# Even and odd sums made after the transposes; six of twelve row tiles kept transposed in DRAM for the rotation

## The chip, the cores and the metric

The kernel runs on one core of a Trainium2 chip. The metric is the device time of one launch in microseconds (us), as the median of several runs. The engines are called TensorE (PE in the profile, with PEld for its weight loads), VectorE (DVE), ScalarE (ACT), GpSimd (Pool) and SyncE (SP), which only issues DMAs here. Each takes its own instructions in order and waits on semaphores for the others.

## The reference

Eight images of 256 channels and 96 x 96 pixels go through two residual layers, all in float32:

```python
x = x + _L0_conv_ref(_gn(x), ...)     # group norm, then attention in the Fourier domain
x = x + _L1_conv_ref(_gn(x), ...)     # group norm, then linear attention
```

Layer 0 makes q, k and v by 256 x 256 matrices over the channels, takes a two-dimensional FFT of each, normalises every channel of q and k over all frequencies, forms 32 x 32 attention matrices per head and takes the softmax of their real and imaginary parts apart:

```python
attn = jnp.einsum('bhcn,bhdn->bhcd', q_f, k_f) * temperature
attn = complex(softmax(real(attn)), softmax(imag(attn)))
out = abs(ifft2(einsum('bhcd,bhdn->bhcn', attn, v_f)))
return pconv(out, w_out)
```

Layer 1 projects x to 32 channels of q and k with softplus, sums k times v over all pixels, and divides q times that sum by q times the sum of k.

## The kernel before, in words

No FFT is computed. The products of q and k over all frequencies without conjugation are, in space, products of x with x mirrored in both axes. So layer 0 needs two 256 x 256 matrices of the image, the second moments of its even part (x plus x mirrored) and of its odd part (x minus x mirrored). The imaginary part of the attention needs a second image y, which is x with every pair of a row and its columns turned by a fixed table of 96 x 96 for each row ("rotation").

One image x lies in an arena of SBUF, channels on 128 partitions in two halves (`KC = 2`), in twelve tiles of 8 rows (`NT`). A tile t holds four rows from the top and the four that mirror them (`x_col`), so a tile carries its own mirror, and tile 0 also the row 48, which mirrors itself. The second arena holds y, and is given to the next image in turn. `ring` (4 buffers of 1536 elements), `three` (3 buffers), `one` and `xT` (6 slots of 2 x 258) are SBUF buffers; `psum` has five banks for all transposes and products but the long sums.

The stages of one image are Python generators, woven together so that TensorE gets work of one stage while another waits:

- `pair_sums(b)`: L313 to L318 add and subtract the mirrored halves of a tile on VectorE or Pool (`even_odd`), L350 transposes 128 pixels of both (4 transposes, "eoT"), L353 copies them to `xT` on ScalarE, and L331 adds their products with themselves to the two sums ("acc"). The products of a step are issued one step behind its transposes. There are 37 steps for an image: three for each of twelve tiles, and one for row 48. `stats_chunk` takes the statistics of the group norm along the way.
- `attention(b)` turns the two sums into the matrices of the heads, a chain of small products and steps of VectorE and ScalarE. Its `yield n` says how many steps of rotation go between its pieces.
- `rotate(b)`: a step takes two rows. L550 transposes each row (2 transposes a row, "xr"), L563 copies them to `xT` on ScalarE, and two steps later L553 multiplies them by the row's table ("y", two passes for each float32 product), and L558 and L559 copy row sums and y from PSUM on VectorE. The table of six rows is a tile "tm", read as overlapping windows of the DRAM tensor `rt` (576 pieces of 384 bytes), with a last column put in by Pool (L536).
- `images(b)`: the products z (L621), squares and roots on VectorE, ScalarE and Pool, and the projection po (L633), added to x.
- `layer1(b)` and `output(b)`: layer 1 in the same arena; L779 transposes x again ("xT"), L782 and L784 copy it on ScalarE or VectorE. `output` adds the result to x on VectorE (L868) and, for one of four pieces, on ScalarE and Pool (L871, L872), and stores it (L882).

`weave` runs image b's attention with its own rotation; `pair_sums(b + 1)` is woven into `images(b)`, `layer1(b)` and `output(b)`, and what is left follows bare. Every stage issues the loads of the next image on SP as space comes free. Where `tc.manual_schedule` names an engine, its instructions stand in the order of the program; elsewhere a planner orders them by when it thinks that they are ready. Attention and rotation have TensorE's order by hand; output and the rest of the sums have TensorE, VectorE, Pool and SP by hand, and ScalarE by the planner; images and layer1 have all by the planner. The sums of the first image stand alone at the start, with VectorE by hand.

Of the kernel before, what the change touches and what calls it, by code (L numbers as in the profile page):

```python
# [54 lines left out]
KC = 2  # L56
# [3 lines left out]
TR = 6  # L60
NZ = 33
# [7 lines left out]
def two_layer_kernel(ctx: ExitStack, tc: tile.TileContext, x, w1t, b1, w2t, b2, w3, b3, wot, temp,  # L69
# [96 lines left out]
    turn = [0, 0]  # L166

    def xt_slot(sums=False):

        turn[sums] += 1  # L170
        return xT[:, NX - 2 + turn[1] % 2 if sums else turn[0] % (NX - 2)]
# [8 lines left out]
    half = const.tile([P, 1], F32, name="half")  # L180
    nc.vector.memset(half, 1.0)
    nc.vector.memset(half[0:W], 0.5 ** 0.5)
# [46 lines left out]
    rt = dram.tile([H, 2 * W], F32, name="rt")  # L229

    def tables():

        nc.vector.reduce_sum(rep4[:, 0:D], ident.rearrange("p (j d) -> p d j", d=D), axis=AX.X)
        for j in range(1, 4):
            nc.vector.tensor_copy(rep4[:, 32 * j:32 * j + 32], rep4[:, 0:D])
        nc.vector.tensor_copy(sel8.rearrange("p (i d) -> p i d", d=D), rep4[:, 0:8].unsqueeze(2).to_broadcast([P, 8, D]))
        for j in range(4):
            o = HEAD * j
            nc.vector.tensor_copy(gsel[:, 0:16, j], gri[:, o:o + 16])
            nc.vector.tensor_copy(gsel[:, 17:32, j], gri[:, P + o + 1:P + o + 16])  # L240
            nc.vector.tensor_copy(gsel[:, 32, j:j + 1], gri[:, o + 16:o + 17])
        pcs = ps_tile("pcs")
        for c in range(2):
            nc.tensor.matmul(pcs[0:H, c:c + 1], lhsT=csn[0:1, c, :], rhs=ones[0:1, 0:1], start=True, stop=True)
        cs = t0[:, 5 * W:5 * W + 2]
        nc.vector.tensor_copy(cs, pcs[0:H, 0:2])
        r0 = t0[:, 2 * W:3 * W]
        nc.vector.tensor_scalar_mul(t0[:, 0:W], t0[:, 0:W], cs[:, 0:1])
        nc.vector.scalar_tensor_tensor(r0, in0=t0[:, W:2 * W], scalar=cs[:, 1:2], in1=t0[:, 0:W], op0=ALU.mult, op1=ALU.add)
        for i in range(2):  # L250
            o = (3 + i) * W
            nc.vector.tensor_copy(t0[:, o:o + 1], r0[:, 0:1])
            nc.vector.tensor_copy(t0[:, o + 1:o + W], r0[:, W - 1:0:-1])
        nc.sync.dma_start(out=rt, in_=t0[:, 3 * W:5 * W])
        load_small()

    def window(h):

        v = rt[h:h + TR, 1:1 + W]
        return bass.AP(v.tensor, v.offset, [[1, W], [2 * W, TR], [1, W]])  # L260
# [35 lines left out]
    def even_odd(b, u):  # L296

        assert (b, u % NT) in loaded
        nr = PR if u < NT else 1
        t = ring_tile(f"eo_{b}_{u}").rearrange("p (c k n) -> p c k n", c=2, k=KC)  # L300
        x_t = image(x_of(b))
        rows = [PR * u + i for i in range(nr)]
        if u in (0, NT):
            parts = [(0, 1)] + ([(1, nr)] if nr > 1 else [])
        else:
            parts = [(0, nr)]
        for lo, hi in parts:
            n = hi - lo
            ra = x_col(rows[lo]) // W
            rp = x_col((H - rows[lo]) % H) // W  # L310
            back = slice(rp, rp - n if rp >= n else None, -1)
            for c in range(2):
                eng = nc.vector if u in (0, 1, NT) or (u == NT // 2 - 1 if b else u % 2) else nc.gpsimd  # L313
                op = (eng.tensor_add, eng.tensor_sub)[c]
                pop = (nc.gpsimd.tensor_add, nc.gpsimd.tensor_sub)[c]
                d = t[:, c, :, 0:nr * W].rearrange("p k (h w) -> p k h w", w=W)
                op(d[:, :, lo:hi, 1:W], x_t[:, :, ra:ra + n, 1:W], x_t[:, :, back, W - 1:0:-1])  # L317
                pop(d[:, :, lo:hi, 0:1], x_t[:, :, ra:ra + n, 0:1], x_t[:, :, back, 0:1])  # L318
        return t, nr * W

    s0 = {}

    def pair_sums(b):

        st0 = new_stats(f"st0_{b}")
        acc = [acc_tile(f"acc{c}_{b}") for c in range(2)]

        def products(t, np_, first, last):
            for c in range(2):
                for m in range(KC):  # L330
                    mm = nc.tensor.matmul(acc[c][:, m * C:m * C + (KC - m) * P], lhsT=t[0:np_, c, m * P:(m + 1) * P],  # L331
                                          rhs=t[0:np_, c, m * P:C], start=(first and m == 0), stop=(last and c == 1),
                                          skip_group_check=True)
                    if first and m:
                        tc.keep_in_program_order(mm)

        pending, first = None, True
        us = [*range(NT - 1, -1, -1), NT]
        ahead = [even_odd(b, us.pop(0))]
        for u in range(NT - 1, -2, -1):  # L340
            u %= NT + 1
            eo, cols = ahead.pop(0)
            for i in range(0, cols, P):
                while i == 0 and us and len(ahead) < (2 if b and u in (NT - 3, NT - 4) else 1):
                    ahead.append(even_odd(b, us.pop(0)))
                np_ = min(P, cols - i)
                pt = ps_tile(f"eoT_{b}_{u}_{i}")
                for c in range(2):
                    for k in range(KC):
                        nc.tensor.transpose(pt[0:np_, c * C + k * P:c * C + (k + 1) * P], eo[:, c, k, i:i + np_], ident)  # L350
                t = xt_slot(True)
                weight = half[0:np_] if u in (0, NT) and i == 0 else 1.0
                nc.scalar.activation(t[0:np_, :, 0:C], pt[0:np_, :].rearrange("p (c n) -> p c n", c=2), AF.Copy,  # L353
                                     scale=weight)
                if pending is not None:
                    products(*pending, first, False)
                    first = False
                pending = (t, np_)
                if u < NT and i:
                    stats_chunk(st0, b, 2 * (NT - 1 - u) + i // P - 1)  # L360
                yield
        s0[b] = st0, acc, products, pending
# [4 lines left out]
    def attention(b):  # L367
        st0, acc, products, pending = s0.pop(b)
        wl = ring_tile(f"wl_{b}").rearrange("p (k o) -> p k o", k=KC)
        nc.sync.dma_start(out=wl[:, :, 0:C], in_=w1t.rearrange("(k p) o -> p k o", p=P))  # L370
        nc.sync.dma_start(out=wl[:, :, C:2 * C], in_=w2t.rearrange("(k p) o -> p k o", p=P))
        nc.sync.dma_start(out=wl[:, :, 2 * C:3 * C], in_=w3.rearrange("(k p) i -> p k i", p=P))
# [14 lines left out]
        yield 2  # L387
# [80 lines left out]
        yield 3  # L468

        for m in range(KC):  # L470
# [15 lines left out]
            yield (5, 3)[m]  # L486
# [38 lines left out]
    def rotate(b):  # L525
# [6 lines left out]

        def load_r(h):
            tm = three.tile([P, TR * (W + 1)], F32, tag="tm", name=f"tm_{b}_{h}")[0:W].rearrange("p (r w) -> p r w", r=TR)
            (nc.scalar if b else nc.sync).dma_start(out=tm[:, :, 0:W], in_=window(h))
            nc.gpsimd.tensor_copy(tm[:, :, W:W + 1], csn[0:W, 2, h:h + TR].unsqueeze(2))  # L536
            return tm

        def step(h, turned):
# [3 lines left out]
            if turned is not None:  # L543
                g, gt, tm = turned
                pu = ps_tile(f"y_{b}_{g}")
            for r in range(2):
                for k in range(KC):
# [3 lines left out]
                    if turned is not None and g + r:  # L551
                        o = (r * KC + k) * (W + 1)
                        nc.tensor.matmul(pu[:, o:o + W + 1], lhsT=gt[0:W, r, k * P:(k + 1) * P], rhs=tm[:, g % TR + r, :],  # L553
                                         start=True, stop=True)
            if turned is not None:
# [3 lines left out]
                nc.vector.tensor_copy(y[:, :, :, g + r:g + 2], src[:, :, W - 1::-1, r:2])  # L559
            if h is not None:  # L560
                xt = xt_slot()
                r = 0 if h else 1
                nc.scalar.copy(xt[0:W, r:2, 0:C], pt[0:W, r * C:2 * C].rearrange("p (r n) -> p r n", n=C))  # L563
                return xt

        tms = [load_r(g) for g in range(0, 3 * TR, TR)]
        pending = []
        for h in range(0, H, 2):
            if h % TR == 0:
                tm = tms.pop(0)  # L570
            if h % TR == 4 and 3 * TR <= h - 4 + 2 * TR < H:
                tms.append(load_r(h - 4 + 2 * TR))
            xt = step(h, pending.pop(0) if len(pending) == 2 else None)
            pending.append((h, xt, tm))
# [5 lines left out]
    st1s = {}  # L580

    def images(b):
# [26 lines left out]
        nc.vector.tensor_mul(sg[2], sg[2], sg[2])  # L609

# [69 lines left out]
    def layer1(b):  # L680
# [72 lines left out]
        def add_kx(i, xt, kT):  # L753
# [4 lines left out]
        extra = [three.tile([P, TR * (W + 1)], F32, tag="tm", name=f"xt{i}_{b}")[:, 0:2 * (C + 2)].rearrange(  # L758
            "p (j n) -> p j n", j=2) for i in range(2)]
        for t in extra:  # L760
            nc.gpsimd.memset(t[:, :, C:C + 2], 1.0)
        slots = [*(xT[:, i] for i in range(4)), *extra]
        pend = []
        softplus(0, 0)
        for s in range(NS):
# [6 lines left out]
            for i in range(s * CH // P, (s + 1) * CH // P):  # L772
                xt = [slots[2 * (i % 3) + jj] for jj in range(2)]
                for jj in range(2):
# [6 lines left out]
                    if jj or i % 3 == 2:  # L781
# [116 lines left out]
    with tc.manual_schedule(engines={mybir.EngineType.DVE}):  # L898
# [67 lines left out]
```

## Time and profile before

| | us |
|---|---|
| median of 3 runs (2762.49 to 2765.9) | 2763.46 |
| the profiled execution | 2762.53 |
| its span, first to last instruction | 2760.7 |
| one image to the next, from the first z at 1170.5 to that at 1509.8 | 339.3 |
| TensorE transposes xr (L550), number | 1520 |
| TensorE passes y (L553), number | 3040 |

The page gives busy time of the engines, the chain of work that ended last, and groups of instructions by source line. The stages of the image in the middle lie at 1170 to 1300 us (images), to 1382 (layer1), to 1432 (output and the bare sums) and to 1510 (attention and rotation). Matmuls overlap in the array, so a mean duration of a matmul is longer than the time from one to the next; the pace is read from starts. "eoT", "acc", "xr" and so on are the names of the tiles that a group writes.

### The profile page before, as it was taken

The page shows a single profiled execution, that of the slowest core. Times are in us where ns is not written, and L with a number is a line of the kernel's source. Part 1 is how long each engine was busy: PE and PEld are TensorE (multiplying, and loading weights), DVE is VectorE, ACT ScalarE, POOL GpSimd, SP SyncE. Part 2 cuts the span into 40 slices and gives each one's busy share as a digit, 9 for nine tenths or more (in the row PEclk, how much of TensorE's full clock was granted, in tenths as well). Part 3 has the DMA queues.
Part 4 walks back from the last instruction along what each step waited for, and adds up shares of the span by engine and source line. Part 5 has one row for each costly group of instructions (what it writes and reads, how often), then busy time and mean ns, then how long its engine had stood idle before and what let it go on. Part 6 is the DMA issues. An engine that isn't in the chain of part 4 may idle for free.

```text
span 2760.7 us, 47785 instructions
## 1 busy us (share of the span) xinstructions
PE 2719.5 (99%) x18348; PEld 1972.5 (71%) x18348; DVE 1958.4 (71%) x4104; ACT 1366.5 (49%) x2098; POOL 841.5 (30%) x939
## 2 busy tenths in 40 slices
PE   8999999999999999999999999999999999999988
PEld 8965679657795677956679566885678856788556
DVE  7588666876668767587675875769766687676776
ACT  3455634556345563355634546345453455544553
POOL 5033340342403423035230351313513135131311
PEclk9999999999999999999999999999999999999997
DMA  5120151201512015120151201521015210251003
GB/s 169 40 65 11 47 184 43 67 9 49 179 43 73 6 47 182 43 69 6 54 179 46 63 6 54 182 54 52 7 53 184 58 46 7 62 178 28 0 7 138
DMA packets 197274, 192.50 MB, mean 70 GB/s; under 512 B 88821, under 2 KB 197049, under 8 KB 197049
## 3 DMA queue, kind: packets, MB, share of 16 engines
q1 hardware_dynamic: 129800, 164.34, 18.8%
q10 hardware_dynamic: 67248, 25.12, 3.6%
q8 instruction: 146, 2.39, 0.4%
q14 instruction: 80, 0.65, 0.1%
HBM read 113.85 MB, written 75.57 MB: 69 GB/s over the span
## 4 chain that ended last, share of the span: by engine, by line
PE 94%; DVE 3%; ACT 2%; DMA 1%; issue 1%; POOL 0%; SPq 0%; POOLq 0%; DVEq 0%; ACTq 0%
PE z L621 21%; PE po L633 18%; PE acc L331 13%; PE y L553 10%; PE xr L550 6%; PE eoT L350 5%; PE xT L779 5%; PE kq L718 5%; PE o L863 4%; PE kx L755 3%; DMA arena<-in_x_dram 1%; PE cw L423 1%; PE kT L770 1%; DVE arena L559 1%; PE mz L511 1%
## 5 line engine op out<-in xcount | busy, mean ns | idle before, releaser
L621 PE MATMUL z<-arena,mz 128*128 128x384 f32 (+2 forms) x2400 | 595.0, 476 | 0.0
L633 PE MATMUL po<-e,wo 128*128 128x384 f32 x1536 | 529.7, 486 | 0.2 <-ACT e L668 0.2
L667 POOL TENSOR_TENSOR e<-e 128x768 f32<-128x768 f32 x192 | 348.2, 1815 | 554.1 <-ACT e L666 554.1
L621 PEld LDWEIGHTS z<-arena,mz 128*128 128x128 f32 (+1 forms) x2400 | 325.6, 163 | 241.4 <-issue 42.4
L553 PE MATMUL y<-tm,xT 96*128 96x97 f32 x3040 | 472.6, 261 | 1.7 <-ACT sd_a L288 0.5
L553 PEld LDWEIGHTS y<-tm,xT 96*128 96x128 f32 x3040 | 457.8, 192 | 12.5 <-issue 4.9
L331 PE MATMUL acc<-xT 128*128 128x256 f32 (+2 forms) x2368 | 440.5, 328 | 3.5 <-ACT xT L353 3.5
L633 PEld LDWEIGHTS po<-e,wo 128*128 128x128 f32 x1536 | 289.4, 190 | 197.7 <-DVE arena L635 1.2
L662 DVE TENSOR_TENSOR e<-z,xT 128x768 f32<-128x768 f32 x384 | 365.7, 953 | 85.2 <-PE z L621 85.2
L264 DVE BATCH_NORM_STATS2 st<-arena 128x6 f32<-128x384 f32 x768 | 406.5, 552 | 13.7 <-DMA arena<-in_x_dram 3.2
L550 PE MATMUL xr<-ident,arena 128*96 128x128 f32 x1520 | 409.2, 275 | 0.0
L331 PEld LDWEIGHTS acc<-xT 128*128 128x128 f32 (+1 forms) x2368 | 380.2, 191 | 37.7 <-ACT xT L353 5.2
L563 ACT COPY xT<-xr 96x512 f32<-96x512 f32 (+1 forms) x384 | 220.2, 578 | 293.8 <-PE xr L550 289.4
L666 ACT ACTIVATE e<-e 128x1536 f32<-128x1536 f32 x192 | 284.6, 1482 | 93.5 <-DVE e L662 92.3
L668 ACT ACTIVATE e<-e 128x768 f32<-128x768 f32 x192 | 161.9, 843 | 334.0 <-POOL e L667 332.9
L317 POOL TENSOR_TENSOR eo<-arena 128x760 f32<-128x760 f32 x136 | 246.1, 1809 | 253.7 <-issue 130.1
L635 DVE TENSOR_TENSOR arena<-arena,po 128x384 f32<-128x384 f32 x384 | 211.1, 551 | 92.6 <-PE po L633 69.5
L353 ACT ACTIVATE xT<-eoT 128x512 f32<-128x512 f32 x280 | 166.6, 598 | 183.9 <-PE eoT L350 182.2
L550 PEld LDWEIGHTS xr<-ident,arena 128*96 128x96 f32 x1520 | 227.2, 150 | 10.3 <-issue 6.9
L559 DVE COPY arena<-y 128x384 f32<-128x384 f32 (+1 forms) x384 | 209.7, 547 | 1.2 <-issue 0.5
L558 DVE COPY ys<-y 128x4 f32<-128x4 f32 (+1 forms) x384 | 62.4, 162 | 199.3 <-PE y L553 195.9
L350 PE MATMUL eoT<-ident,eo 128*128 128x128 f32 (+1 forms) x1184 | 188.1, 280 | 10.4 <-POOL eo L318 10.4
(202 smaller groups left out, 2907.0 us busy)
## 6 DMA issues: line engine op xcount, KB each, us to landing
arena<-in_x_dram SPq DMA_DIRECT2D x184, 384.0 KB
out_dram<-arena SPq DMA_DIRECT2D x184, 384.0 KB
tm<-rt ACTq DMA_DIRECT2D x112, 216.0 KB
tm<-rt SPq DMA_DIRECT2D x16, 216.0 KB
arena<-in_x_dram SPq DMA_DIRECT2D x8, 288.0 KB
out_dram<-arena SPq DMA_DIRECT2D x8, 288.0 KB
wl<-in_w1t_dram SPq DMA_DIRECT2D x8, 256.0 KB
wl<-in_w2t_dram SPq DMA_DIRECT2D x8, 256.0 KB
```

The source lines that it names most:

```text
L264: nc.vector.bn_stats(out=st[:, k, c, :], in_=x_of(b)[:, k, c * CH:(c + 1) * CH])
L317: op(d[:, :, lo:hi, 1:W], x_t[:, :, ra:ra + n, 1:W], x_t[:, :, back, W - 1:0:-1])
L331: mm = nc.tensor.matmul(acc[c][:, m * C:m * C + (KC - m) * P], lhsT=t[0:np_, c, m * P:(m + 1) * P], rhs=t[0:np_, c, m * P:C], start=(first ...
L350: nc.tensor.transpose(pt[0:np_, c * C + k * P:c * C + (k + 1) * P], eo[:, c, k, i:i + np_], ident)
L550: nc.tensor.transpose(pt[0:W, r * C + k * P:r * C + (k + 1) * P], x_of(b)[:, k, o:o + W], ident)
L553: nc.tensor.matmul(pu[:, o:o + W + 1], lhsT=gt[0:W, r, k * P:(k + 1) * P], rhs=tm[:, g % TR + r, :], start=True, stop=True)
L559: nc.vector.tensor_copy(y[:, :, :, g + r:g + 2], src[:, :, W - 1::-1, r:2])
L621: mm = nc.tensor.matmul(out[:, o:o + n * W], lhsT=columns(mz, k, c, j), rhs=y[:, k, h * W:(h + n) * W], start=(k == 0 and o == 0), stop=(k ...
L633: nc.tensor.matmul(po[:, 0:CH], lhsT=wo[:, k, m * P:(m + 1) * P], rhs=e[:, k, :], start=(k == 0), stop=(k == KC - 1))
L662: nc.vector.tensor_add(e[:, 2 * c:2 * c + 2, :].rearrange("p t (q h) -> p t q h", h=H), pz[:, 0:CH].rearrange("p (q h) -> p q h", h=H).uns ...
L666: nc.scalar.activation(e, e, AF.Square)
L667: nc.gpsimd.tensor_add(e[:, 0:2, :], e[:, 0:2, :], e[:, 2:4, :])
```

## The change

Four things change together.

1. The sums. The two halves of a tile are transposed first, x as it lies and its mirror through a reversed copy (`back`); Pool makes that copy, or ScalarE for the tiles 5 to 0 of all images but the first. ScalarE then copies both from PSUM to a tile of `ring` (`both`), with a weight for each partition (`pw`), and only then come sum and difference: on VectorE, from PSUM and `both`, or on Pool, from `both` alone. Which engine makes which is said by `pool`: in the first image, and in the last five steps of each, VectorE makes the sum and Pool the difference; else tiles 11 to 9 and two of three steps of tiles 5 to 0 go to Pool alone, the others to VectorE alone. The first column of every row, which mirrors within itself, is collected in `w0`; it and the rows 0 and 48 share the last two steps of tile 0 in pieces of 16 or 32 pixels. There are still 37 steps.
2. The spill. In all images but the first, what the tiles 11 to 6 (the rows 24 to 71 without 48) have as transposed x and mirror is written from `both` to DRAM (`xtd`), two DMAs of 128 KB a step; their first column goes there through one more transpose (`w0T`). Rotation doesn't transpose these 46 rows again: `fetch` reads a pair of rows on SP into a slot of `xT` three steps ahead.
3. Rotation. The pieces of six rows are taken in another order, with pieces that are fetched and pieces that are transposed in turn; it uses all six slots of `xT`. The mirrored rows come with their pixels reversed and use a second table, `rb`. The finished table tiles of the first images are stored in DRAM (`rx`) and later read in 96 long pieces. All these loads go to SP's queue (before, ScalarE's for all images but the first).
4. Small moves. `wl` is loaded near the end of the sums; the two buffers for layer 1's transposes get their ones in `images`; of the 36 transposed pieces of x in layer 1, ScalarE copies 30 (before, 24) and VectorE 6 (12); three `yield`s of `attention` are longer; Pool is ordered by hand in the first sums too.

The diff, cut to its core:

```diff
+    pw = const.tile([P, 4], F32, name="pw")
...
-            (nc.scalar if b else nc.sync).dma_start(out=tm[:, :, 0:W], in_=window(h))
+            turned = H // 2 <= h < H - PR * T0
+            if b > turned:
+                nc.sync.dma_start(out=tm, in_=rx[h // TR])
+                return tm
...
+        def turn_back(i):
+            t, j = steps[i]
...
+            ab = sides(t, j)
+            ready = len(ab) == 1
+            front = ab[0][2] if ready else xts[-1][:, j % 3, 0].rearrange("p (k n) -> p k n", k=KC)
+            for p0, n, *v in ab:
+                for c in range(ready, 2):
+                    if v[c] is not None:
+                        (nc.scalar.copy if b and t < T0 and (ready or not c) else nc.gpsimd.tensor_copy)(
+                            (front, back[:, i % 2])[c][:, :, p0:p0 + n], v[c])
+            return front, xts[-1][:, j % 3]
...
+        for i, (t, j) in enumerate(steps):
+            front, both = ahead
+            if i + 1 < len(steps):
+                ahead = turn_back(i + 1)
+            pt = ps_tile(f"eoT_{b}_{t}_{j}").rearrange("p (c n) -> p c n", c=2)
+            for k in range(KC):
+                nc.tensor.transpose(pt[:, 0, k * P:(k + 1) * P], front[:, k], ident)
+                nc.tensor.transpose(pt[:, 1, k * P:(k + 1) * P], back[:, i % 2, k], ident)
+            nc.scalar.activation(both, pt, AF.Copy, scale=pw[:, j:j + 1])
+            if b and t >= T0:
+                n = P - j // 2
+                for c in range(2):
+                    nc.sync.dma_start(out=turned(c, PR * t, 1 + P * j)[0:n], in_=both[0:n, c])
+            eo = sum_slot()[:, :, 0:C]
+            pool = (j if t < T0 else t > NT - 4) if b and i < len(steps) - 5 else None
+            for c, (op, on_pool) in enumerate(((ALU.add, nc.gpsimd.tensor_add), (ALU.subtract, nc.gpsimd.tensor_sub))):
+                if pool or pool is None and c:
+                    on_pool(eo[:, c], both[:, 0], both[:, 1])
+                else:
+                    nc.vector.scalar_tensor_tensor(eo[:, c], in0=pt[:, 0], scalar=pw[:, j:j + 1], in1=both[:, 1],
+                                                   op0=ALU.mult, op1=op)
...
+        pieces = [TR * i for i in (15, 4, 0, 5, 14, 6, 1, 8, 13, 7, 2, 9, 12, 10, 3, 11)]
...
+        def fetch(i):
+            if i < len(order) and spilled(order[i]):
+                xts[i] = xT[:, i % NX]
...
+                nc.sync.dma_start(out=xts[i][0:W, :, 0:C], in_=rows.rearrange("(r w) n -> w r n", w=W))
...
+            step(None if spilled(h) else h, pending.pop(0) if len(pending) == 2 else None, xts[i])
+            pending.append((h, xts.pop(i), tm))
+            fetch(i + 3)
...
-                    if jj or i % 3 == 2:
+                    if jj or i % 6 > 1:
                         nc.scalar.copy(xt[jj][:, :, 0:C], src)
...
-    with tc.manual_schedule(engines={mybir.EngineType.DVE}):
+    with tc.manual_schedule(engines={mybir.EngineType.DVE, mybir.EngineType.Pool}):
```

## The prediction

> **What bounds the kernel now.** I read the page first: busy shares and the chain of work that ended last.
>
> ```profile
> PE 2719.5 (99%) x18348; PEld 1972.5 (71%) x18348; DVE 1958.4 (71%) x4104; ACT 1366.5 (49%) x2098; POOL 841.5 (30%) x939
> ...
> PE 94%; DVE 3%; ACT 2%; DMA 1%; issue 1%; POOL 0%; SPq 0%; POOLq 0%; DVEq 0%; ACTq 0%
> PE z L621 21%; PE po L633 18%; PE acc L331 13%; PE y L553 10%; PE xr L550 6%; PE eoT L350 5%; PE xT L779 5%; PE kq L718 5%; PE o L863 4%; PE kx L755 3%; DMA arena<-in_x_dram 1%; PE cw L423 1%; PE kT L770 1%; DVE arena L559 1%; PE mz L511 1%
> ```
>
> TensorE is nearly the whole chain. Modelled ends make PE busy look fuller than it is, so I also looked at starts in the timeline of one image (1170 to 1510 us): where two lie over 0.45 us apart, what is above 0.15 adds up to 2.5 us. Next the stretches of that image, between output and rotation, and one table load in rotation (columns: length, busy of PE, PEld, DVE, ACT, POOL, clock, DMA share, GB/s).
>
> ```profile
> 1395.00:1431.00 36.00, 36.00 (x258) 27.92 (x258) 29.57 (x61) 13.85 (x25) 22.25 (x27) 1.00 0.94 326
> 1440.00:1510.00 70.00, 69.43 (x641) 65.52 (x643) 41.59 (x139) 28.41 (x53) 2.73 (x16) 1.00 0.18 45
> ...
> 1452.70:1453.20 0.50, 0.50 (x7) 0.50 (x6) 0.15 (x1) 0.00 (x0) 0.00 (x0) 1.00 0.00 1
> 1453.20:1453.70 0.50, 0.50 (x7) 0.50 (x5) 0.24 (x2) 0.38 (x1) 0.00 (x0) 1.00 0.60 94
> 1454.20:1454.70 0.50, 0.50 (x5) 0.46 (x5) 0.00 (x0) 0.00 (x0) 0.00 (x0) 1.00 0.33 90
> ```
>
> Output fills the DMA engines (0.94); rotation leaves them at 0.18. The table load was issued at 1452.22, moved its first bytes after 1453.2 and was done before 1454.7: at most 2.5 us for 576 packets. Then the groups that the change touches (busy us, mean ns; the second form of L353 is the one with a scale per partition):
>
> ```profile
> L553 PE MATMUL y<-tm,xT 96*128 96x97 f32 x3040 | 472.6, 261 | 1.7 <-ACT sd_a L288 0.5
> L550 PE MATMUL xr<-ident,arena 128*96 128x128 f32 x1520 | 409.2, 275 | 0.0
> L317 POOL TENSOR_TENSOR eo<-arena 128x760 f32<-128x760 f32 x136 | 246.1, 1809 | 253.7 <-issue 130.1 <-PE eoT L350 117.1 <-POOL eo L318 5.6
> L353 ACT ACTIVATE xT<-eoT 128x512 f32<-128x512 f32 x280 | 166.6, 598 | 183.9 <-PE eoT L350 182.2
> L353 ACT ACTIVATE xT<-eoT,half 128x512 f32<-128x512 f32 x8 | 5.5, 687 | 12.2 <-PE eoT L350 12.2
> ```
>
> A mean of 275 ns is a latency, not the pace. The pace of a rotation step (two rows) is seen where the last steps turn from transposes and products to products alone:
>
> ```profile
> 1164.37 0.17 DVE L558 COPY ys<-y 128x4 f32<-128x4 f32 x1 [0.61 <-PE y L553]
> 1165.60 0.16 DVE L558 COPY ys<-y 128x4 f32<-128x4 f32 x1 [0.61 <-PE y L553]
> 1166.84 0.16 DVE L558 COPY ys<-y 128x4 f32<-128x4 f32 x1 [0.61 <-PE y L553]
> 1167.73 0.16 DVE L558 COPY ys<-y 128x4 f32<-128x4 f32 x1 [0.27 <-PE y L553]
> 1168.62 0.16 DVE L558 COPY ys<-y 128x4 f32<-128x4 f32 x1 [0.27 <-PE y L553]
> ```
>
> With four transposes a step takes 1.236 us (1164.37 to 1166.84, halved), without them 0.89.
>
> [...] eight passes of y alone take 0.89 us, 111 ns each, though only 97 columns move; [...] here (1815 - 1004) / (768 - 384) = 2.11 ns from L667 and L872. [...] here a VectorE L317 of 128x760 took 5.56 us beside Pool (at 18.05) where two took 1.82 at 6.19. [...]
>
> **The change, part by part.**
> Rotation, seven images: 23 pairs of rows (24 to 71 but for 48 and 49) lose four transposes and a ScalarE copy: 23 x (1.236 - 0.89) = 8.0 us an image, 56 in all. VectorE needs 0.16 + 0.55 a step and has had 41.59 of 70 us; in 62 that is 67%, so it stays cover. In exchange 23 fetches of 192 packets of 1 KB come in on SP. No such fetch exists; the nearest is the 2.5 us table load. A fetch is issued when step i-1 has freed its slot and used in step i+5: with alternating pieces 3 x 0.89 + 3 x 1.236 = 6.4 us ahead. Zero, if it lands in 2 to 6 us. The table loads move from ScalarE's queue to SP, behind the last output stores; these drain at 1431, the first y needs a table near 1436: zero to 2 us an image, I take 0.
> Spills: 36 stores of 128 KB and two of 24 KB per image, on SP, from sums 0 to 17. Counting the yields (3 in images, 15 in layer1) these all come before output, where the share of DMA was 0.03 to 0.31; 4.7 MB over 80 us is 59 GB/s. At 0.5 us of issue each they take 19 us of SP; loads of the next x wait behind them but are needed later: zero, unless a store waits long at the head of SP. Two more transposes per image: 2 x 0.11 x 7 = 1.5 us.
> Sums, 37 steps an image: as many transposes (4) and products (8 passes) as before: 0.44 + 1.31 = 1.75 us of TensorE. Around them a longer path:
>
> ```profile
> 1426.21 0.60 PE L350 MATMUL eoT<-ident,eo 128*128 128x128 f32 x4
> 1426.64 1.47 PE L331 MATMUL acc<-xT 128*128 128x256 f32 x8
> 1426.91 0.69 ACT L353 ACTIVATE xT<-eoT,half 128x512 f32<-128x512 f32 x1 [1.15 <-PE eoT L350]
> ```
>
> ScalarE begins 0.27 after the transposes' end and takes 0.69 with the scale. Then VectorE's sum, 256 elements from PSUM (estimate 0.45, from 0.55 for 384 in L635), and beside it Pool's difference: 1004 - 128 x 2.11 = 0.73. With 0.1 for handing over: 1.55 us to the even products, against 1.31 + 0.44 = 1.75 until they are due; the odd ones are due 0.65 later and ready at 1.85. No stall where both engines share. Where Pool does both, even is ready at 1.9 and odd at 2.6, against 1.75 and 2.4 in a bare run, 2.7 and 3.3 in output, where o adds 0.93. Pool's own time: a reversed copy (0.65, from 0.52 for 192 elements in L530), 0.73 and small columns (0.15) make 1.5 of 1.75 in image 0; at the end of images 0.65 + 2 x 0.73 = 2.1 a step, six steps 12.7 of the 16.6 us between 1297.9 and 1314.5; in output, where ScalarE makes the copy, L872's 1.0 + 2 x 0.73 = 2.5 of 2.76 in two of three steps. The work hiding all this is the products one step behind; without that cover the path's 1.55 would add to each step. Removed: Pool's L317 and L318 before the transposes. I take a loss at the narrow pieces of tile 0 (four to nine small copies on Pool and ScalarE, 0.3 each) and the last product: 0.5 us x 8, and 2 more in image 0, where Pool makes them all: 6.
> layer1: six x copies go from VectorE to ScalarE (0.59 each; ScalarE 23.88 of 42 us), a transposed tile keeps its PSUM bank until VectorE has summed: 0 to 2 an image, I take 0.5 x 7 = 3.5. The weights wl come some steps sooner, kxt moves its two Pool memsets (0.1 us), longer yields give the attention chain more steps in front of each product: zero. New constants on VectorE at the start, some 20 of 0.06 us, lie before x lands at 6 us: zero.
> Sum: -56 + 1.5 + 6 + 3.5 = -45. On the profiled span of 2760.7 that is 2716; the run lies 1.8 above its span and the median 0.9 above that: **2718**, the own range 2700 to 2733.
>
> **Rivals.**
> Half: pieces late by 0.1 us in 296 steps, or an attention chain (VectorE, ScalarE) that shows as rotation shrinks, give back 20 to 40 us: 2735 to 2757. For it: Pool at 90% in output. Against: 37 x 0.1 must fall in steps that have up to 0.9 spare.
> More: the three waits of 1 us for tile 0's load and other PE gaps go too, and a transpose is worth 109 ns: 23 x 4 x 0.109 x 7 = 70, so 2690.
> Unchanged: the fetches set the pace. 48 steps are eight turns of six slots, the gain of 8.0 is 1.0 a turn: break-even at 7.4 us from slot free to used, 2763. Against: 2.5 us at 0.18 share.
> Slower: the sums' path becomes the bound. Place: transposes, ScalarE, one engine for both sums, product. Each product waits for transposes of one step before, so the pace is (path + 1.75) / 2. The 45 are eaten from 0.15 us a step over all 296, or 0.37 over the 121 bare ones. A path of 2.6 to the even products makes 2.18: in bare steps 121 x 0.43 = 52, so 2770; in all of them 2763 - 45 + 127 = 2845. For it: a strict chain of three engines in place of one copy. Against: bare steps are 37 of image 0 and some 12 of each later image, and only few of them have Pool do both.
>
> **How the numbers follow.** Likeliest 0.50, half 0.18, more 0.06, unchanged 0.06 (within 0.2%, 5.5 us, about what a measurement can tell from no change), slower 0.20. Faster is 0.74. Of the slower fifth I take in a third, up to 2778; below I stop at 2698.
>
> **What would show it.** y steps in rotation near 0.89 and 1.24 in turn, xr count 1520 - 644 = 876; per-image period 339.4 to about 333; fetches landed within 3 us. Wrong if acc or eoT shows waits of PE on POOL or ACT in output and bare sums, if y waits for a fetch, or if SP holds an x load back past its step.

## The result

The changed kernel takes 2750.84 us (median of 4 runs, 2746.7 to 2754.01) against 2763.28 us for the kernel before (4 runs, 2762.49 to 2765.9): a ratio of 0.9952, 95% interval 0.9935 to 0.997. The profiled execution took 2752.79 us with a span of 2751.0. So 12 us were gained where 45 were forecast. From one image to the next (first zs to first zs, mean of seven) it is 337.8 us after 339.8, where about 333 were forecast.

The page of the changed kernel, its busy line and the two groups of rotation:

```profile
PE 2683.0 (98%) x17718; PEld 1934.7 (70%) x17718; DVE 1969.0 (72%) x4247; ACT 1363.9 (50%) x2167; POOL 851.9 (31%) x1252
...
L653 PE MATMUL y<-tm,xT 96*128 96x97 f32 x3040 | 424.1, 268 | 3.6 <-ACT xT L662 2.9
...
L650 PE MATMUL xr<-ident,arena 128*96 128x128 f32 x876 | 229.3, 275 | 0.0
```

The xr transposes fell from 1520 to 876. All idle time ahead of the 3040 y products is 3.6 us, and no DMA is among its releasers. (The chain that ended last breaks off early in this profile: its shares add up to 2%. It is not used here.) Two starts in the timeline of a fetched piece of rotation, and a window over most of one rotation (length, busy of PE, PEld, DVE, ACT, POOL, clock, DMA share, GB/s):

```profile
1440.12 0.16 DVE L658 COPY ys<-y 128x4 f32<-128x4 f32 x1 [0.35 <-PE y L653]
1441.01 0.17 DVE L658 COPY ys<-y 128x4 f32<-128x4 f32 x1 [0.27 <-PE y L653]
```

```profile
1435.00:1500.00 65.00, 64.58 (x562) 60.82 (x563) 42.69 (x148) 20.00 (x39) 0.51 (x4) 1.00 0.40 113
```

A step without transposes takes 0.89 us, TensorE is busy for 64.58 of 65 us, and the DMA share has risen from 0.18 to 0.40 without a wait. The gain is all there. To see what took it back, I cut both profiles at the same events: first xr (rotation), first zs (images), first kq (layer 1), first o (output) of each image (us, means of the seven images that have the stage; the o stage runs to the next image's first xr and so holds output and the bare sums):

| stage | before | after | difference | in 7 images |
|---|---|---|---|---|
| attention and rotation (images 1 to 7) | 73.70 | 65.64 | -8.06 | -56.4 |
| images | 146.0 | 146.0 | 0 | 0 |
| layer 1: first kq to first o | 73.34 | 75.69 | +2.35 | +16.4 |
| output and bare sums: first o to next xr | 46.81 | 50.42 | +3.61 | +25.3 |
| image 0's own sums; last image from its first zs | | | | +1.9; +2.7 |

The sum is -10.1, against -9.7 between the two spans. So 46 us come back, where the prediction had 11. (The last image is not read further: in the nine kernels that follow the one before it takes from 1.2 us less to 3.0 more, in no order that the edits explain.) The waits view names the places. Total, times, longest (us), before and then after:

```profile
PE acc L331 <- ACT xT L353: 3.5, 7, 0.5
```

```profile
PE acc L329 <- DVE xT L411: 17.7, 19, 1.6
...
PE acc L329 <- POOL xT L409: 17.2, 15, 3.0
```

The products, which hardly waited before, now wait for their sums: rarely, but for up to 3 us. The largest wait lies in the bare run, at the same step of each image: the product of sum 31 (counted from 0; it is of tile 1), which is due between the transposes of sum 32 and those of sum 33. From the first of these transposes to the second took 3.83 to 6.35 us, 4.81 on average, against 1.94 before. This is called the step after sum 31 below. The timeline of the changed kernel there:

```profile
1419.49 0.27 PE L398 MATMUL eoT<-ident,back 128*128 128x128 f32 x1
...
1420.91 0.27 PE L397 MATMUL eoT<-ident,arena 128*128 128x128 f32 x1
...
1422.05 0.24 ACT L383 COPY xt<-arena 128x64 f32<-128x64 f32 x1 [3.01 <-DMA arena<-in_x_dram]
1422.20 0.68 ACT L399 ACTIVATE xt<-eoT,pw 128x512 f32<-128x512 f32 x1
...
1423.02 1.41 POOL L409 TENSOR_TENSOR xT<-xt 128x256 f32<-128x256 f32 x2 [3.83 <-ACT xt L399]
...
1423.80 1.71 PE L329 MATMUL acc<-xT 128*128 128x256 f32 x5 [2.29 <-POOL xT L409]
...
1426.16 0.42 PE L397 MATMUL eoT<-ident,arena 128*128 128x128 f32 x1
```

The transposes of sum 32 start at 1420.91, those of sum 33 at 1426.16. Sum 31's are done at 1419.8. Its copy (L399) could go then, but ScalarE stands for 3.01 us at a narrow copy of tile 0 (L383, 64 elements), which belongs to a step four sums later and waits for tile 0's load. ScalarE takes its instructions one after the other, and outside the engines ordered by hand a planner had put the narrow copy first. Pool's sums are late after it (3.83), and TensorE after them (2.29).

In layer 1 one place is the table load ahead of the first logarithms. Before, then after:

```profile
656.31 1.28 ACT L746 ACT_TABLE_LOAD   x1
...
658.63 1.06 ACT L353 ACTIVATE xT<-eoT 128x512 f32<-128x512 f32 x2
...
659.26 1.46 PE L331 MATMUL acc<-xT 128*128 128x256 f32 x7 [0.50 <-ACT xT L353]
```

```profile
654.96 1.28 ACT L854 ACT_TABLE_LOAD   x1
...
657.28 1.24 ACT L399 ACTIVATE xt<-eoT,pw 128x512 f32<-128x512 f32 x2
...
658.36 0.86 DVE L411 SCALAR_TENSOR_TENSOR xT<-eoT,pw,xt 128x256 f32<-128x256 f32 x2
...
658.88 1.57 PE L329 MATMUL acc<-xT 128*128 128x256 f32 x8 [1.56 <-DVE xT L411]
```

Both kernels have ScalarE's copies behind the table load and two logarithms. Before, the copy was the last link to the product; now two sums on VectorE follow it, and the wait grows from 0.50 to 1.56 us. Not all of this stays: by the first product for the divisor of layer 1 (den, L926) the changed kernel is 0.53 us late, counted from the first kq. The larger part of the stage's 2.35 comes after that.

The last thing that the comparison shows lies on SP's queue (start, and time over which the grouped issues run). The first line is the output stores before, the others are the changed kernel:

```profile
1393.75 2.56 SPq L882 DMA_DIRECT2D out_dram<-arena  x4
```

```profile
1378.88 3.21 SPq L403 DMA_DIRECT2D xtd<-xt  x4
1387.57 5.62 SPq L432 DMA_DIRECT2D xtd<-xt  x2
...
1393.63 2.61 SPq L986 DMA_DIRECT2D out_dram<-arena  x4
```

and in the windows of the time in which SP stands at L432:

```profile
1381.50:1387.50 6.00, 6.00 (x36) 3.79 (x35) 4.30 (x11) 1.67 (x5) 0.00 (x0) 1.00 0.07 24
1387.50:1393.00 5.50, 5.50 (x43) 3.96 (x41) 4.21 (x10) 2.74 (x7) 4.78 (x8) 1.00 0.09 30
```

The column transfers (L432) write over rows that the spills have written, so they wait for these. From 1382 to 1393 SP stands there, but for the issue of the first of the two, with the output stores and the next loads behind it, and the DMA engines are nearly empty: a share of 0.07 is one of sixteen (0.0625). In the 4 us from 1382 the trace has 94 packets of 1 KB at 46 ns, 4.3 us of one engine's time. They are the spills of 127 rows (84 of the 252). SP's own waits in the whole run say the same (total, times, longest):

```profile
SPq L432 <- DMA xtd<-xt: 71.8, 14, 5.4
```

The first output store is issued 8.4 us after the first o product (1385.22), before the change 5.6 (1388.13).

### The profile page after: what moved, and what is told of

Same layout as the page of the kernel before. It is cut to its first block, busy times and chain, and to the rows that moved or that the text cites. A ratio compares the mean times of both kernels' runs of the same rounds, so it can differ in the third digit from the quotient of the medians.

```text
span 2751.0 us, 47847 instructions
## 1 busy us (share of the span) xinstructions
PE 2683.0 (98%) x17718; PEld 1934.7 (70%) x17718; DVE 1969.0 (72%) x4247; ACT 1363.9 (50%) x2167; POOL 851.9 (31%) x1252
## 5 line engine op out<-in xcount | busy, mean ns | idle before, releaser
L329 PE MATMUL acc<-xT 128*128 128x256 f32 (+1 forms) x2368 | 451.4, 332 | 34.9 <-DVE xT L411 17.7
L329 PEld LDWEIGHTS acc<-xT 128*128 128x128 f32 x2368 | 385.0, 193 | 79.8 <-DVE xT L411 26.0
L653 PE MATMUL y<-tm,xT 96*128 96x97 f32 x3040 | 424.1, 268 | 3.6 <-ACT xT L662 2.9
L653 PEld LDWEIGHTS y<-tm,xT 96*128 96x128 f32 x3040 | 411.8, 192 | 16.5 <-issue 7.4
L399 ACT ACTIVATE xt<-eoT,pw 128x512 f32<-128x512 f32 x296 | 202.6, 687 | 159.9 <-PE eoT L398 153.6
L409 POOL TENSOR_TENSOR xT<-xt 128x256 f32<-128x256 f32 x324 | 235.6, 744 | 88.2 <-ACT xt L399 82.8
L662 ACT COPY xT<-xr 96x512 f32<-96x512 f32 (+1 forms) x223 | 127.3, 575 | 249.6 <-PE xr L650 249.1
L650 PE MATMUL xr<-ident,arena 128*96 128x128 f32 x876 | 229.3, 275 | 0.0
L411 DVE SCALAR_TENSOR_TENSOR xT<-eoT,pw,xt 128x256 f32<-128x256 f32 x268 | 118.7, 475 | 121.5 <-ACT xt L399 121.5
L972 DVE TENSOR_TENSOR arena<-arena,o 128x384 f32<-128x384 f32 x288 | 142.5, 549 | 37.8 <-PE o L967 37.8
```

The source lines that it names most:

```text
L409: on_pool(eo[:, c], both[:, 0], both[:, 1])
L650: nc.tensor.transpose(pt[0:W, r * C + k * P:r * C + (k + 1) * P], x_of(b)[:, k, o:o + W], ident)
L653: nc.tensor.matmul(pu[:, o:o + W + 1], lhsT=gt[0:W, 1 - r if back else r, k * P:(k + 1) * P], rhs=tm[:, g % TR + r, :], start=True, stop=True)
```

## The experiments

Theory: two causes made the difference to the forecast. ScalarE's order puts a copy that waits for a load ahead of the sums; and the spills, by way of SP, make this load late. The rivals were one cause alone, and lengths of the chain that no order mends.

**ScalarE by hand.** The changed kernel with ScalarE among the engines that the output stage orders by hand.

```diff
-        with tc.manual_schedule(engines={... EngineType.Pool, mybir.EngineType.SP}):
+        with tc.manual_schedule(engines={... EngineType.Pool, mybir.EngineType.SP, mybir.EngineType.Activation}):
```

> The changed kernel, but ScalarE too in the order of the program during output and the bare sums. Theory A (in all seven images ScalarE's planned order has copies of tile 0's narrow pieces, which wait for tile 0's load, ahead of its copy of sum 31): the wait of TensorE behind sum 31, 2.1 to 4.6 us an image and 21 us in all, shrinks to at most 1 us an image, attention and rotation stay at 65.6 us, so some 15 to 20 us less than the changed kernel: 2731 to 2736. Theory B (the load itself lands too late, because spills, fetches and wl crowd the queue): the products wait as long, only at a later step: within 4 us of the changed kernel. Theory C (Pool making both halves is too slow a path): the same wait at sum 31, no change.

Measured: 2737.39 us (4 runs, 2735.93 to 2738.18), ratio to before 0.9899 [0.9882, 0.9915]. The step after sum 31 takes 1.79 us in all images; first o to next xr fell from 50.42 to 48.37 us, times 7 is 14.4, about as much as the whole run gained. The two programs differ in the order of ScalarE's instructions alone, so this order was a cause, as theory A has it; the time lies 1 us above its range. In the kernel before, the planned order of ScalarE is the hand order already, so this cost came with the change. What is left of the late load shows one step further on (2.99 us on average, 1.99 before), in this timeline of the same image:

```profile
1418.27 0.40 ACT L383 COPY back<-arena 128x256 f32<-128x256 f32 x1 [3.00 <-DMA arena<-in_x_dram]
...
1418.58 0.68 ACT L399 ACTIVATE xt<-eoT,pw 128x512 f32<-128x512 f32 x1
1418.73 0.33 PE L398 MATMUL eoT<-ident,back 128*128 128x128 f32 x1 [0.83 <-ACT back L383]
```

ScalarE waits just as long for tile 0, but no other step's copy is behind it now, and TensorE loses 0.83 us.

**No spill.** The changed kernel in which rotation transposes all rows again and nothing goes to DRAM and back.

```diff
-            if b and t >= T0:
+            if False:
...
-            if b and (t, j) == (T0, 2):
+            if False:
...
-            return b > 0 and PR * T0 <= h < H - PR * T0 and h != H // 2
+            return False
```

> The changed kernel without spill and fetch: all rows are transposed again in rotation, the sums stay as changed. By all theories attention and rotation go back from 65.6 to about 73.7 us in seven images, 57 us. Theory A: nothing else changes, the wait behind sum 31 stays at 2 to 4.6 us, so 2751 + 57 = 2808 (2800 to 2815), which makes the sums' part of the change alone some 45 us slower than the kernel before. Theory B: with no spill the load lands sooner, the wait behind sum 31 shrinks below 1 us: 2785 to 2792.

Measured: 2791.62 us (2 runs), ratio 1.0096 [1.0076, 1.0117]. This is the rest of the change alone, above all the sums made after the transposes: it loses some 27 us, and the spill then gains 41. By stage: layer 1 has nearly its whole loss without any spill (75.52 against 75.69 us); first o to next xr is 48.40 instead of 50.42; the step after sum 31 is 2.79 instead of 4.81 us. The time lies in theory B's range. So by way of the late load the spill costs 2 us an image at this step, and the wait behind ScalarE's order is there without it, but small (0.85 over the kernel before). Attention and rotation go back to 73.35 us and not to 73.70: 0.35 us of the gain there came with the other parts of the change.

**128 rows.** The changed kernel with the spill of each tile's third step made one row longer; the row holds zeros and is overwritten by the column transfer. The buffer in DRAM grows with it, so its second half lies at other addresses; no engine's order changes.

```diff
-    xtd = dram.tile([2, (H // 2 - PR * T0) * W, C], F32, name="xtd")
+    xtd = dram.tile([2, (H // 2 - PR * T0 + 1) * W, C], F32, name="xtd")
...
-                n = P - j // 2
+                n = P
...
-                    nc.sync.dma_start(out=xtd[c].rearrange("(h w) n -> h w n", w=W)[:, 0], in_=col[o:o + n])
+                    nc.sync.dma_start(out=xtd[c].rearrange("(h w) n -> h w n", w=W)[0:n, 0], in_=col[o:o + n])
```

> The changed kernel, with the spilled transposes of the third step of each tile stored as 128 rows instead of 127 (the 128th row is zeros, and the column transfer writes over it). Theory A: the 127-row transfers, which run on one of the 16 DMA engines at a share of 0.07, hold back the column transfers, these hold back SP's first output stores by 2.8 us, and so tile 0's load is late. Then the stores start 5.3 to 5.8 us after the first output product instead of 8.4, the step after sum 31 takes about 2.8 us instead of 4.8 on average, and the time is 2737 us (2733 to 2741). Theory B: the lateness comes from the bytes and issues of the spills, not from their shape: stores at 7.5 us or later, time 2747 to 2752 us.

Measured: 2737.56 us (4 runs, 2734.88 to 2740.09), ratio 0.9903 [0.9888, 0.9918]: one row more in 84 transfers is worth 13 us. SP's queue in the same image:

```profile
1374.68 1.89 SPq L403 DMA_DIRECT2D xtd<-xt  x4
1377.53 0.79 SPq L432 DMA_DIRECT2D xtd<-xt  x2
...
1386.29 2.72 SPq L986 DMA_DIRECT2D out_dram<-arena  x4
```

SP's waits at the column transfers in the whole run, 71.8 us in the changed kernel:

```profile
SPq L432 <- DMA xtd<-xt: 6.5, 7, 1.1
```

The column transfers are issued 1 us after the spills and no longer last into the output stage; the stores start 5.3 us after the first o. The step after sum 31 takes 2.47 us on average. The bytes are the same but for 0.8% of a third, so the shape was the cause. With 127 rows the share is 0.07, one engine's, and 127 packets at 46 ns make 5.8 us for one such transfer. With 128 rows, in the window behind the issue of the four spills above, the share is 0.57, as much as nine engines at full use:

```profile
1376.00:1378.00 2.00, 2.00 (x12) 1.54 (x12) 1.83 (x5) 0.30 (x1) 0.00 (x0) 1.00 0.57 195
```

What makes the two so different no run shows.

**Both.** The edits of the first and third experiment together.

> The edit of 128 rows and ScalarE by hand in the output stage, together. Theory A (two causes, ScalarE's order and the late load): the waits of 0.7 to 1.5 us for tile 0's load that were left with ScalarE by hand go too, 7 images by 1.3 us, so 2728 us (2724 to 2731). Theory B (one cause, either edit removes it): 2735 to 2738 us, as with ScalarE by hand alone.

Measured: 2733.46 us (4 runs, 2730.75 to 2735.27), ratio 0.9887 [0.9873, 0.9902]. It is below each edit alone by 4 us and above the 2728 of the theory: there are two causes, but each edit alone removes most of what they cost together. That fits the picture: a load that comes in time does no harm at the head of ScalarE, and a load that is late does little where no other step's copy stands behind it. So the 128 rows are worth 13 us in the planner's order of ScalarE and 4 in the hand order. First o to next xr: 47.76 us, after 48.37 and 48.18 for one edit each; the step after sum 31 takes 1.80 us and the next one 2.36.

**The last sum.** In the profile with ScalarE by hand the last product of an image waits for a sum that stands behind the aggregation of the statistics:

```profile
1425.74 1.45 DVE L296 BATCH_NORM_AGGREGATE mv_a<-st 128x2 f32<-128x144 f32 x2
...
1427.58 1.58 PE L329 MATMUL acc<-xT 128*128 128x256 f32 x8 [0.89 <-DVE xT L411]
```

The kernel of both edits, with one more:

```diff
-            nc.vector.bn_aggr(out=mv[:, k, :], in_=st[:, k, :, :].rearrange("p n s -> p (n s)"))
+            aggr = nc.vector.bn_aggr(out=mv[:, k, :], in_=st[:, k, :, :].rearrange("p n s -> p (n s)"))
+            if name[0] == "a":
+                tc.keep_in_program_order(aggr)
```

> The kernel of 128 rows and ScalarE by hand, and VectorE's aggregation of the statistics (1.45 us) held behind the last sum instead of ahead of it. Theory A: the last product no longer waits 0.9 us for its sum, 7 images by 1.0 us less: 7 us under the kernel without this edit, 2721 us (2717 to 2725). Theory B: the aggregation's result is then late for the group means and the rotation's first steps wait in its place: within 2 us of the kernel without it.

Measured: 2728.3 us (4 runs, 2726.76 to 2729.62), ratio 0.9871 [0.9855, 0.9888], 5 us less than without the edit, above theory A's range and below B's. The sum now stands ahead of the aggregation:

```profile
751.25 0.48 DVE L413 SCALAR_TENSOR_TENSOR xT<-eoT,pw,xt 128x256 f32<-128x256 f32 x1 [0.44 <-ACT xt L401]
751.65 1.46 DVE L296 BATCH_NORM_AGGREGATE mv_a<-st 128x2 f32<-128x144 f32 x2
```

The stage is 0.69 us shorter (47.07), 4.8 us in seven images; attention is unchanged at 65.68, so the later result of the aggregation cost nothing there. From the last sum's transposes to the first xr it is 3.38 us, after 4.08 without this edit and 3.06 before the change; 0.32 us stay.

**Sums on Pool; no w0T.** Two runs on layer 1's loss, each against the kernel of the last sum.

```diff
-            pool = (j if t < T0 else t > NT - 4) if b and i < len(steps) - 5 else None
+            pool = (j if t < T0 else t > NT - 4 or (t == T0 and j)) if b and i < len(steps) - 5 else None
```

> The kernel of the last-sum edit (2728.3 us), with the sums of the two steps before the output stage, (6, 1) and (6, 2), taken from VectorE to Pool. Theory A: the output stage starts 2.9 us later after the reciprocal's row sums than before the change because VectorE has four sums (1.65 us) ahead of its first normalization; Pool stands idle there for 4.9 us. Then the first output product comes 0.8 to 1.2 us sooner in each of 7 images: 2721 us (2718 to 2724). Theory B: the delay is the w0T transposes and the PSUM buffer that they hold, so VectorE's sums don't matter: 2726 to 2730 us.

```diff
-                pt = ps_tile(f"w0T_{b}")
-                col = xts[-2][:, 0, 0]
-                for k in range(KC):
-                    nc.tensor.transpose(pt[0:H + 1 - PR * T0, k * P:(k + 1) * P], w0[:, k, PR * T0:H + 1], ident)
-                nc.scalar.copy(col[0:H + 1 - PR * T0], pt[0:H + 1 - PR * T0, 0:C])
+                col = both[:, 0]
```

> The kernel of the last-sum edit (2728.3 us), without the w0T transposes and their copy: the column transfers take rows of the step's own transposes in their place, so the column w = 0 of the spilled rows is not that of x and this part of the computation is left out. Theory A (VectorE's four sums delay the output stage): only the 0.4 us of the two transposes on TensorE goes, 2725 to 2728 us. Theory B (w0T and its PSUM buffer delay it): 1.0 to 1.5 us sooner in each of 7 images, 2718 to 2722 us.

Measured: Pool sums 2722.81 us (4 runs, 2722.24 to 2725.37), ratio 0.9848 [0.9832, 0.9864]; no w0T 2722.5 us (4 runs, 2721.3 to 2724.91), ratio 0.9849 [0.9834, 0.9863]. Both times lie in or beside the range of one theory, but by the stages neither cause has the size that its theory gives it. With Pool's sums the first o comes 2.34 us sooner after the first rec, but the first rec comes 2.15 later: what moved is the mark, since the products of the step before now stand ahead of rec. From first kq to first o it is 75.71 to 75.52 us, 0.19 an image where 0.8 to 1.2 were expected; another 0.39 came after the first o. The first o moves as a mark too: the next transposes start 2.19 us behind it before the change, 1.85 after it, and 1.64 with Pool's sums. Counted from the first kq to these transposes, layer 1 takes 75.54 us before the change, 77.53 after it, 77.57 with the last sum's edit and 77.16 with Pool's sums: the loss is 1.99 us an image (and that of the output stage 3.95), and Pool's sums give back 0.41. Without w0T the same stretch is 75.48 (0.23 less), the one after it 0.24 less; that is 3.3 us of the 5.5 between the two profiled spans, the rest lies in image 0 and in the last image. So w0T costs about half a microsecond an image at most. Each is a part of layer 1's loss, and neither is the reason for the whole.

**Logarithms behind.** The kernel of Pool sums, with the first two logarithms held behind the copies.

```diff
-            nc.scalar.activation(u, u, AF.Ln, bias=zero)
+            ln = nc.scalar.activation(u, u, AF.Ln, bias=zero)
+            if c == 0 and s < 2:
+                tc.keep_in_program_order(ln)
```

> The kernel of Pool sums (2722.8 us), with the first two logarithms of layer 1 and the table load ahead of them (1.28 us) kept behind the two ScalarE copies that stood after them. Theory A (layer 1's part of the loss is one longer chain, copy on ScalarE and then two sums on VectorE, behind the table load): the products of that step no longer wait, 0.7 to 1.1 us sooner in 7 images, 2715 to 2718 us. Theory B (the logarithms are themselves awaited): the transposes of k wait in the products' place, by the 1.3 us of the two copies less what the products gave back, 2722 to 2728 us.

Measured: 2720.16 us (4 runs, 2717.97 to 2723.5), ratio 0.9837 [0.9821, 0.9853], between the two theories. Two lines of its timeline:

```profile
651.76 0.69 ACT L401 ACTIVATE xt<-eoT,pw 128x512 f32<-128x512 f32 x1 [0.66 <-PE eoT L400]
...
656.77 0.55 PE L878 MATMUL kT<-ident,arena 128*128 128x128 f32 x3 [0.58 <-DVE arena L860]
```

The copy now runs as soon as its transposes are done, and no product waits at this place. But the transposes of k wait for the logarithm in their stead, and 0.66 us an image is left of the gain (74.86 from first kq to first o). Both waits stand behind one table load. This is the fastest of the versions: 1.6% below the kernel before, 31 us below the changed one.

What is left of layer 1's loss is 1.5 us an image to the first o, or 0.96 to the transposes after it (76.50 us). By den the last kernel is as early after the first kq as the kernel before, 65.02 against 65.06 us, so what the table load had cost has come back. The rest arises one step later, around the products that spread the divisor's reciprocal (rec). Before, then the last kernel:

```profile
1383.34 0.60 PE L350 MATMUL eoT<-ident,eo 128*128 128x128 f32 x4
1383.77 1.47 PE L331 MATMUL acc<-xT 128*128 128x256 f32 x8
1385.18 0.93 PE L839 MATMUL rec<-rec,sel 32*128 32x384 f32 x8
```

```profile
1365.23 0.27 PE L399 MATMUL eoT<-ident,arena 128*128 128x128 f32 x1
...
1366.32 1.61 PE L331 MATMUL acc<-xT 128*128 128x256 f32 x8 [0.49 <-POOL xT L411]
...
1367.77 0.38 PE L430 MATMUL w0T<-ident,w 128*73 128x128 f32 x2
1368.08 0.93 PE L947 MATMUL rec<-rec,sel 32*128 32x384 f32 x8
```

The product starts 1.09 us after the first of the transposes ahead of it, before the change 0.43; 0.49 of this is TensorE idle behind Pool's sums. From the product to rec it is 1.76 instead of 1.41, with the transposes of w0T in between. No run took these two apart in this kernel.

## Why the prediction was right or wrong

- **Rotation, -56 us: right.** 8.06 us an image measured, 8.0 forecast. By the run without spill 7.71 of this belong to the rows that are fetched, 84 ns for each transpose; the prediction priced it at 87, from the pace of 1.236 and 0.89 us. The rival that took 109 ns, the 6% of the chain over 1520 transposes, is refuted.
- **Fetches and table loads, zero: right.** No y product waited for a DMA; the share rose to 0.40. The rival "unchanged" falls.
- **Output with Pool making both sums: right.** Its steps take 2.75 us as before. The rival "slower", a path that sets the pace of every step, falls: most bare steps keep 1.75. VectorE's new sums (L411, from PSUM and SBUF) took 412 to 486 ns in all 268 cases, 0.45 us estimated; the 26 of them with Pool at work all the while (L383, L409) took at most 485, so none waits as the L317 of 5.56 us did.
- **"Two more transposes per image", 1.5 us: right in kind.** Taking them and their copy out gave 3.3 us by stages.
- **Spills, "zero, unless a store waits long at the head of SP": failed, by its own condition.** The column transfer waits there for 127-row spills that run on one DMA engine (share 0.07). The working took 4.7 MB over 80 us and the share of 16 engines; it didn't ask over how many engines one transfer is spread (0.07 for 127 rows, 0.57 for 128). The price was some 13 us (128 rows), of which some 9 came by way of ScalarE's order.
- **"The narrow pieces of tile 0 and the last product", 0.5 us x 8: the term that failed most.** Measured are 3.61 us an image from first o to next xr, 25 in all, the late load included. The copies' own durations were priced, and each is as short as estimated (0.24). What was left out is where they stand: on ScalarE, ahead of other steps' copies, and tied to the load that lands last. The last product's part is 1.06 us an image, twice the whole term. A path that no later product covers, the prediction's picture, fits at most the 0.32 that stayed; 0.70 was an order once more, the aggregation ahead of the last sum on VectorE.
- **Layer 1, 0.5 us x 7: failed in size and in cause.** Measured 2.35 an image to the first o, 16.4 in all. The term was for the x copies moved to ScalarE and for PSUM banks held longer. With the logarithms behind, den comes as early as before the change with those copies where the change put them, so up to there no cost of them is seen. The step that failed is the cover: the prediction asked whether the engines have time in layer 1, and took the products one step behind to cover the sums' path everywhere. At the table load this cover was used up already before the change (the wait of 0.50). There the wait grew by 1.06 us, 0.53 of it still stood at den, and order gave 0.66 back. At rec the product waits for its sums again; Pool's sums gave 0.41 back, leaving out w0T 0.23, each alone. The rest is open.
- **Image 0, 2 us: right** (1.9).
- **The signs.** Of those that the prediction named, two for being wrong came true: acc waits on Pool in the bare sums, and SP holds an x load back.
- **The rivals.** "Half" has the right time (2735 to 2757) by luck, with a wrong picture: not 0.1 us in each of 296 steps, nor an attention chain, but a few places in each image with 0.5 to 4.6 us each. With most of these causes removed, 2720 us are reached. That this is near the 2718 of the sum is in part luck too: the edits go beyond the change, and layer 1 still loses some 10 us to the first o where 3.5 were forecast, while the output stage loses nothing where 3.5 were.

## What to carry to other kernels

A path that the work one step behind covers on average is still bare at the steps where an engine already waits: look in the trace for the waits that exist before the change, and ask there first what each link added to the chain will cost. Here 1.06 us more of waiting left half of that 40 us later. When small instructions move to another in-order engine, price not their durations but what they wait for and what stands behind them. And of each new transfer read from a trace what share of the DMA engines it gets in its shape (here 0.07 with 127 rows and 0.57 with 128), above all when another transfer or a queue waits for it.

## What had not been expected of the hardware

A transfer of 127 rows of 1 KB ran on one DMA engine, 46 ns a packet and so some 5.8 us, at a share of 0.07; with 128 rows the share was 0.57 (2 us behind the issue of four such transfers), and 84 such rows more made the kernel 13 us faster, or 4 us where ScalarE was ordered by hand. A copy of 64 elements on ScalarE takes 0.24 us, and cost up to 4.6 us by its place in the queue.
